# An early x1 buffer for the last block of the finished batch, one gap more per block, and another bank for the first feed-forward product

## The chip, the cores and the metric

The kernel runs on one core of a Trainium2 chip. The metric is the device time of one execution in microseconds. Before the change three runs took 2745.36, 2745.53 and 2747.55 us; the median is 2745.53 us. One further execution, of 2746.23 us, was recorded by the profiler, and everything that is read from a profile below is read from that one.

## The reference

Two batches of 512 channels by 2048 tokens (64 x 32 positions), all in fp32, go through two layers.

```python
x = conv_attention(x)                      # layer 0: softmax attention, 8 heads of 64, + residual
t = tokens(x)
t = t + attn(norm(t))                      # layer 1: Nystrom attention, 256 landmarks
t = t + ffn(norm(t))                       # two linear maps 512 -> 512, no nonlinearity between

# attn, per head: qL, kL are means of 8 tokens each of q and k
attn1 = softmax(q @ kL.T); attn2 = softmax(qL @ kL.T); attn3 = softmax(qL @ k.T)
z = pinv(attn2, 6 iterations)              # xz = a @ z; z = z/4 @ (13 I - xz (15 I - xz (7 I - xz)))
out = attn1 @ (z @ (attn3 @ v)) + conv33(v)
out = out @ Wout + bout
```

The kernel works with channels on the partitions and tokens along the free axis. The two maps of the feed-forward are multiplied into one matrix `mT` beforehand.

## The kernel before

**Stages.** The first half (to about 1500 us) is layer 0; then come the projections of layer 1. From 1733 us a loop goes over eight pairs of heads, `todo`: the four pairs of batch 1 (n = 0 to 3) and then the four of batch 0 (n = 4 to 7). For each pair it runs six iterations of the pseudo-inverse, `Pair.pinv`. This chain is narrow and every step waits for the one before: a transpose of one block on TensorE (line 1528), a copy of it by ScalarE (L1529), eight matmul passes (L1538), two VectorE steps (L1551) that make the next operand. Two heads alternate, so that one head's matmuls run under the other's VectorE steps.

**Turns.** Between the iterations, `pinv` calls `chunk(0)` to `chunk(4)` (called c0 to c4 here), and in the last iteration `last(0)` to `last(5)` (l0 to l5). These calls put other work in: attn1 of the pair before, attn3 and values of the pair after, and the work that ends batch 1. This last work is one generator, `finish1_units`, and each `advance(finish)` moves it by one unit; below, one such call is a *turn*. The generator goes over four blocks of 512 tokens. For each block it emits, turn by turn:

- the load of x1 (the residual) for the block, issued on GpSimd's queue (L1644) into the only buffer of tag `xr`, and two turns that do nothing (`gap(2)`; the load takes the first);
- out.0 to out.3: 8 matmul passes each of the output projection (L968) and one VectorE addition into x1 (L975);
- s0, two VectorE additions (L986, L987), a gap; s1, the mean on TensorE (L990) and its subtraction on VectorE (L991); s2, three squares on ScalarE (L994, L997); s3, three VectorE additions (L1002, L1003), a gap; s4, the variance on TensorE (L1006), its root on ScalarE and the reciprocal on VectorE (L1660);
- map.0 to map.3: 8 matmul passes each of the feed-forward (L1694); the VectorE steps and the store of the result (L1683 to L1685, called rest) come a turn later than their product, and rest.3 runs at the head of the next block's load.

**Order.** TensorE, VectorE, ScalarE and GpSimd each execute in the order in which the Python code emits. Only the order of SyncE's queue, which issues most DMAs, is chosen by the scheduler. An instruction that waits holds up all that follows on its engine.

**The last stage.** After the loop a string gives the order by hand: `1` is a unit of attn1 of the last pair (`last_attn1`), `f` a turn of `finish`, `n` makes the four blocks of batch 0 and issues the loads of their x1 on SyncE, `a`/`b` are their output projections, `s`/`t` the steps of their norms. `n` takes the buffers of batch 1's outputs, and so comes after out.3 of batch 1's last block. Then the blocks of batch 0 go through the feed-forward, their products in banks chosen by `wide_banks`: products 0 and 2 in the two banks of their own, `side_bank(1)` and `side_bank(3)`, products 1 and 3 in the two of `product_bank`. `side_bank(1)` is also the bank of attn1's values (L1611), which L1631 reads.

**Buffers.** PSUM has four banks for general use (`bank`), two `product_bank`, and `side_bank` 1 and 3. In SBUF the tag `v` of `kvpool` has two buffers, used in turn for the keys and the values of the pairs. The values of pair 7, the last, are read for the last time by its convolution, in c4 of pair 6.

Of the kernel before, what the change touches and what calls it, by code (L numbers as in the profile page):

```python
# [10 lines left out]
F32 = mybir.dt.float32  # L11
# [5 lines left out]
P = 128  # L17
# [4 lines left out]
NPAIR = HEADS // 2  # L22
TB = 512
NTB = S // TB
NST = S // P
# [638 lines left out]
def fast_path(  # L664
# [43 lines left out]
    lpool = ctx.enter_context(tc.tile_pool(name="l1", bufs=1))  # L708
    both = ExitStack()
    xpool = both.enter_context(tc.tile_pool(name="x1", bufs=NTB))  # L710
    kvpool = both.enter_context(tc.tile_pool(name="kv1", bufs=2))
# [19 lines left out]
    def bank(name):  # L731
        return ps.tile([P, 512], F32, tag="pp", name=name)
# [11 lines left out]
    def side_bank(i, name):  # L744
        return ps.tile([P, 512], F32, tag=f"av{i}", name=name, bufs=1)

    def product_bank(name):
        return ps.tile([P, 512], F32, tag="pr", name=name, bufs=2)
# [5 lines left out]
    def block_of(pool, tag, name):  # L754
        return pool.tile([P, KC, TB], F32, tag=tag, name=name)
# [37 lines left out]
    def advance(gens, n=1):  # L793


        made, i = 0, 0
        while made < n and i < len(gens):
            got = next(gens[i], gens)
            if got is gens:
                gens.pop(i)  # L800
            elif got is GAP:
                i += 1
            else:
                made += 1
        return made

    def drain(gen):
        for _ in gen:
            pass

    def gap(n=1):
        for _ in range(n):
            yield GAP
# [45 lines left out]
    class Heads0:  # L859
# [61 lines left out]
        def values(self):  # L921
            for t in range(NTB):
                values_of_tokens(self.v, t, self.xbs[t], lambda k: wv_sb[:, k, self.cols], self.name)
                yield
# [107 lines left out]
    def finish0_units(b, oTs, outs_done):  # L1032
        last = None
        for t in range(NTB):
            xb = block_of(lpool, "xr", f"xr_f0_{b}_{t}")
            nc.sync.dma_start(xb, chunked(x[b])[:, :, t * TB : (t + 1) * TB])
            yield from gap()

            for m, _ in enumerate(out0_units(b, t, xb, oTs)):
                if last and m == 0:  # L1040
                    next(last)
                yield
            if t == NTB - 1:
                outs_done.append(True)
            if last:
                yield from gap()
            xn = block_of(lpool, "xn", f"xn_f0_{b}_{t}")
            last = norm0_steps(b, t, xb, xn, xn[:, :2, :])
            next(last)
            yield from gap(2)  # L1050
            next(last)
            yield
            yield from gap(2)
            next(last)
            yield from gap(2)
            next(last)
            yield
        next(last)
# [155 lines left out]
    class Pair:  # L1214
# [310 lines left out]
        def flip(self, X, name):  # L1525
# [3 lines left out]
            nc.scalar.copy(X[:, 1, :P], tp[:, :P])  # L1529

        def pinv(self, chunk, last):


# [167 lines left out]
                yield  # L1701
            rest(*last)

    def finish1_units(b, os):
        for t in range(NTB):
            xb = block_of(lpool, "xr", f"xb_g_{b}_{t}")
            f = Finish1(b, t, os, xb, lambda: block_of(lpool, "xn", f"xn_g_{b}_{t}"), True)
            yield from gap(2)
            yield from f.out_units()
            yield from f.norm_units()  # L1710
            yield from f.map_units(lambda m, name: bank(name))


    todo = [(b, hp) for b in range(B) for hp in range(NPAIR)]
# [3 lines left out]
    oTs, finish, work = [], None, []  # L1718
    for n, (b, hp) in enumerate(todo[:-1]):
# [14 lines left out]
        finish = None  # L1734
# [6 lines left out]
        if hp == NPAIR - 1:  # L1741
            outs_done = []
            finish = finish0_units(b, oTs, outs_done)
# [47 lines left out]
    b = B - 1  # L1791

    def as_block(tile):
        return tile.rearrange("p a b -> p (a b)").rearrange("p (k n) -> p k n", k=KC)
# [60 lines left out]
    todo = pairs[1] + pairs[0]  # L1855
# [28 lines left out]
    def late_buffer(name):  # L1884

        return block_of(xpool, "xb", name).rearrange("p k n -> p (k n)")
# [33 lines left out]

    finish = []
    for n, pair in enumerate(todo):
        before = todo[n - 1] if n else None
        after = todo[n + 1] if n + 1 < len(todo) else None
        if n + 2 < len(todo):
            todo[n + 2].prefetch_w()
        if n == NPAIR + 2:
            before.load_o(kvpool.tile([P, S], F32, tag="k", name=f"o2_{n - 1}"))  # L1930
        if n == NPAIR + 3:
            before.load_o(late_buffer(f"o2_{n - 1}"))
        pair.iteration_start()
        while vals:
            advance(vals)
        if after:
            after.prefetch()
            after.attn3_begin()
        if n + 2 < len(todo):
            vals = [values(n + 2)]  # L1940
        if n:
            q = late_buffer if n > NPAIR + 1 else lambda name: kvpool.tile([P, S], F32, tag="k", name=name)
            pair.prefetch1(q(f"q2_{pair.name}"))

        def chunk(c):
            nonlocal landmarks
            if before and 0 < c <= n_ones:
                before.attn1_end(c - 1)
            if n == NPAIR and c == 1:

                finish.append(finish1_units(1, [p.o for p in todo[:NPAIR]]))
            advance(finish)
            if c == NTB:
                if after:
                    landmarks = after.landmarks_values()
                    next(landmarks)
                    drain(convolution(n + 1))
                else:
                    advance(finish, 2)
                return  # L1960
            ones_before = before if c < n_ones else None
            if ones_before:
                if c:
                    before.attn1_scores(c, 0)
                    before.attn1_scores(c, 1)
                before.attn1_add(c)
            if after:
                for s, bank_of in ((2 * c, product_bank), (2 * c + 1, bank)):
                    after.attn3_scores(s, bank_of)
                    after.attn3_add(s)  # L1970
            else:
                advance(finish)
            if ones_before:
                before.attn1_values(c)
            if after:
                after.attn3_values(2 * c)
            else:
                advance(finish)
            if ones_before:
                before.attn1_sums(c)  # L1980
            if after:
                after.attn3_values(2 * c + 1)
            if ones_before:
                before.attn1_inverse(c)
            if n == NPAIR + 2 and c % 2:
                advance(finish)

        def last(i):
            nonlocal start
            if i == 1 and after:  # L1990
                next(landmarks)
                drain(landmarks)
                start = after.start_values()
            if i == 2 and after:
                next(start)
            else:
                advance(vals)
            if i == 3 and after:
                next(start)
            if n_ones < NTB:  # L2000

                if i == 0:
                    before.attn1_scores(n_ones, 0)
                    before.attn1_scores(n_ones, 1)
                    before.attn1_add(n_ones)
                if i == 1:
                    before.attn1_values(n_ones)
                if i == 2:
                    before.attn1_sums(n_ones)
                if i == 3:  # L2010
                    before.attn1_inverse(n_ones)
                if i == 5:
                    before.attn1_end(n_ones)
            if i == 5:
                pair.attn1_scores(0, 0)
                pair.attn1_scores(0, 1)
            advance(finish)

        landmarks = start = None
        n_ones = NTB if n + 2 < len(todo) else NTB - 1  # L2020
        pair.pinv(chunk, last)

    def last_attn1():
# [15 lines left out]
            yield  # L2039

    def wide_banks(m, name):
        return product_bank(name) if m % 2 else side_bank(1 + m, name)

    def last_block(t):
        xb = as_block(qopool.tile([P, NST, P], F32, tag="qo", name=f"xb_g_0_{t}"))
# [16 lines left out]


    ones_last = last_attn1()
    for c in "11ffnf11f1ff1afafff1f1f1f1faas11bs1bs1bbt":
        if c == "f":
            advance(finish)
        elif c == "n":

            fs = [last_block(t) for t in range(NTB)]  # L2070
            outs = [f.out_units() for f in fs]

            st = [f.steps(deviation_of(t)) for t, f in enumerate(fs)]
        else:
            next(ones_last if c == "1" else {"a": outs[0], "b": outs[1], "s": st[0], "t": st[1]}[c])
# [104 lines left out]
```

## Time and profile before

| | us |
|---|---|
| median of three runs | 2745.53 |
| profiled execution, whole | 2746.23 |
| its span from first to last instruction | 2744.4 |
| TensorE busy | 2698.0 (98%) |
| VectorE busy | 1631.3 (59%) |
| ScalarE busy | 905.5 (33%) |
| GpSimd busy | 161.1 (6%) |

TensorE is busy nearly all the time, so what can be lost or won lies in its short idle stretches, and in the stretches in which its clock is halved. Times in the text are us from the start of the span. Pair 6 starts at 2351 and pair 7 at 2458; the string of the last stage starts at 2574.

### The profile page before, as it was taken

The numbers are of one execution on the slowest core, as the hardware profiler recorded it, in microseconds if no ns is written. First come the engines' busy times: TensorE is split into PE (matmuls) and PEld (weight loads), VectorE is DVE, ScalarE is ACT, GpSimd is POOL, SyncE is SP. The second block draws the span as 40 slices with busy tenths as digits, with TensorE's granted clock in tenths as the row PEclk, the third lists the DMA queues.
The fourth block names the chain that finished last, engine by engine and source line by source line (L and its number), as shares of the span: only waits on it lengthen the run. The fifth ranks groups of instructions, "written<-read, shape, count | busy, mean of one in ns | idle before, by whom it ended". The sixth has DMA issues, their size and how long they took to land.

```text
span 2744.4 us, 41181 instructions
## 1 busy us (share of the span) xinstructions
PE 2698.0 (98%) x16994; PEld 1361.6 (50%) x16994; DVE 1631.3 (59%) x2087; ACT 905.5 (33%) x1352; POOL 161.1 (6%) x109
## 2 busy tenths in 40 slices
PE   9999999999999999999999999999999999998899
PEld 5343443434443334343344455777677666655334
DVE  3768777665558755657667544544644645465455
ACT  1434343433335334445422223233333222221210
POOL 0101101000011100000002000000000000000000
PEclk9999999999999999999999999999999999999999
DMA  4100000212111200012024632213111213020311
GB/s 146 43 9 24 28 20 24 85 36 70 32 66 54 96 24 21 24 41 74 24 88 172 208 122 90 96 34 114 57 36 59 63 41 105 24 70 27 104 39 47
DMA packets 111476, 173.99 MB, mean 63 GB/s; under 512 B 16176, under 2 KB 67888, under 8 KB 106672
## 3 DMA queue, kind: packets, MB, share of 16 engines
q1 hardware_dynamic: 105136, 150.00, 16.8%
q0 software_dynamic: 5440, 20.97, 2.1%
q8 instruction: 135, 2.21, 0.3%
q14 instruction: 61, 0.50, 0.1%
q10 hardware_dynamic: 704, 0.31, 0.0%
HBM read 90.87 MB, written 63.57 MB: 56 GB/s over the span
## 4 chain that ended last, share of the span: by engine, by line
PE 90%; DVE 5%; DMA 2%; SPq 1%; ACT 1%; issue 1%; POOL 0%; DVEq 0%; POOLq 0%; ACTq 0%
PE sc_f L1072 15%; PE av_f L1102 15%; PE pp L1245 8%; PE pb L1538 5%; PE pa L1538 5%; PE vp_f L953 4%; PE vp L953 4%; PE fp_g L1694 4%; PE pp_k_f L905 4%; PE yp_f L968 4%; PE pp_q_f L905 3%; PE yp_g L968 3%; PE sc L1367 2%; PE av L1388 2%; PE sc L1595 2%; DVE acc_f L1090 2%
## 5 line engine op out<-in xcount | busy, mean ns | idle before, releaser
L1090 DVE TENSOR_TENSOR acc_f<-acc_f,p_f 128x1024 f32<-128x1024 f32 x448 | 582.3, 1300 | 209.0 <-ACT p_f L1080 180.4
L1080 ACT ACTIVATE p_f<-sc_f 128x1024 f32<-128x1024 f32 x512 | 496.4, 1021 | 564.2 <-PE sc_f L1072 561.5
L1072 PE MATMUL sc_f<-q_f,k_f 64*64 64x512 f32 x4096 | 491.1, 595 | 2.7 <-ACT p_f L1080 2.7
L1102 PE MATMUL av_f<-p_f,v_f 64*64 64x512 f32 x4096 | 484.3, 589 | 0.0
L1102 PEld LDWEIGHTS av_f<-p_f,v_f 64*64 64x64 f32 x4096 | 156.5, 133 | 283.1 <-issue 283.1
L1072 PEld LDWEIGHTS sc_f<-q_f,k_f 64*64 64x64 f32 x4096 | 145.8, 133 | 285.6 <-issue 262.0
L1245 PE MATMUL pp<-xh,w 128*128 128x512 f32 x512 | 229.1, 600 | 0.7 <-ACT q L1248 0.7
L1245 PEld LDWEIGHTS pp<-xh,w 128*128 128x128 f32 x512 | 95.3, 191 | 121.0 <-issue 113.8
L1538 PE MATMUL pb<-R 128*128 128x192 f32 (+1 forms) x640 | 151.9, 384 | 2.1 <-DVE M L1551 2.1
L1538 PE MATMUL pa<-M 128*128 128x192 f32 (+1 forms) x640 | 150.7, 380 | 1.4 <-ACT M L1529 1.4
L953 PEld LDWEIGHTS vp_f<-wv_f,x 128*128 128x128 f32 x1024 | 115.7, 192 | 13.5 <-issue 11.8
L1538 PEld LDWEIGHTS pb<-R 128*128 128x128 f32 x640 | 108.2, 193 | 25.9 <-DVE M L1551 3.1
L953 PE MATMUL vp<-w,xh 128*128 128x128 f32 x1024 | 120.9, 276 | 0.0
L953 PEld LDWEIGHTS vp<-w,xh 128*128 128x128 f32 x1024 | 117.0, 192 | 7.2 <-issue 4.6
L1538 PEld LDWEIGHTS pa<-M 128*128 128x128 f32 x640 | 108.1, 193 | 21.6 <-ACT M L1529 4.2
L953 PE MATMUL vp_f<-wv_f,x 128*128 128x128 f32 x1024 | 118.8, 277 | 0.0
L968 PE MATMUL yp_g<-o,wo_f 128*128 128x512 f32 x256 | 116.4, 604 | 2.3 <-DVE xb_g L975 2.3
L1694 PE MATMUL fp_g<-xn_g,mT 128*128 128x512 f32 (+1 forms) x264 | 114.4, 583 | 3.2 <-DVE rinv L1631 3.2
L905 PE MATMUL pp_k_f<-x,wk_f 128*128 128x512 f32 x256 | 114.3, 599 | 1.4 <-DVE k_f L908 1.0
L905 PE MATMUL pp_q_f<-x,wq_f 128*128 128x512 f32 x256 | 114.2, 598 | 1.3 <-DVE q_f L908 1.3
L968 PE MATMUL yp_f<-q_f,wo_f 128*128 128x512 f32 x256 | 113.6, 598 | 0.8 <-DVE xr_f L975 0.8
L1120 POOL TENSOR_TENSOR q_f<-q_f,rinv_f 128x512 f32<-128x512 f32 x32 | 46.3, 1445 | 1041.8 <-DMA rinv_f<-acc_f 829.6
(198 smaller groups left out, 2710.4 us busy)
## 6 DMA issues: line engine op xcount, KB each, us to landing
xh<-xh_fd SPq DMA_DIRECT2D x12, 1024.0 KB, 5.4
rinv_f<-acc_f SPq DMA_DIRECT2D x256, 32.0 KB, 1.9
xr_f<-in_x_dram SPq DMA_DIRECT2D x8, 1024.0 KB, 5.4
x_fd<-xr_f POOLq DMA_DIRECT2D x8, 1024.0 KB, 4.9
xh_fd<-xn_f POOLq DMA_DIRECT2D x8, 1024.0 KB, 4.7
k_fd<-k SPq DMA_DIRECT2D x32, 256.0 KB, 2.9
q_fd<-q SPq DMA_DIRECT2D x32, 256.0 KB, 2.8
k<-k_fd SPq DMA_DIRECT2D x8, 1024.0 KB, 6.2
```

The source lines that it names most:

```text
L905: nc.tensor.matmul(pp, lhsT=w_sb[kind][:, k, cols], rhs=xbs[t][:, k, :], start=k == 0, stop=k == KC - 1)
L953: nc.tensor.matmul(vp[:, j * P : (j + 1) * P], lhsT=xb[:, k, j * P : (j + 1) * P], rhs=w_of(k), start=k == 0, stop=k == KC - 1,)
L968: nc.tensor.matmul(yp, lhsT=wo_sb[:, k, m * P : (m + 1) * P], rhs=oTs[k][:, toks], start=k == 0, stop=k == NPAIR - 1,)
L1072: nc.tensor.matmul(sc[r * D : (r + 1) * D, h, :], lhsT=hd.k[rows, lo : lo + D], rhs=hd.q[rows, t * TB : (t + 1) * TB], start=True, stop=True,)
L1080: nc.scalar.activation(p, sc, AF.Exp, scale=D**-0.5)
L1090: nc.vector.tensor_tensor(acc, first if c == 1 else acc, p, ALU.add)
L1102: nc.tensor.matmul(av[r][half, :], lhsT=hd.v[keys, c, half], rhs=pp[keys, h, :], start=c == 0, stop=c == NST - 1,)
L1245: nc.tensor.matmul(pp, lhsT=self.w[j][:, c, :], rhs=xhs[t][:, c, :], start=c == 0, stop=c == KC - 1)
L1367: nc.tensor.matmul(scs[h][:, j * LM : (j + 1) * LM], lhsT=self.k[rows, c * P : (c + 1) * P], rhs=self.L[0][rows, :], start=True, stop=True,)
L1388: nc.tensor.matmul(self.av3[half, :LM], lhsT=self.v[:, c, half], rhs=self.p3[s][:, h, j * LM : (j + 1) * LM], start=c == 0, stop=c == NST - 1,
L1538: nc.tensor.matmul(dst, lhsT=lhsT[:, k, t * P : (t + 1) * P], rhs=rhs[:, k, :], start=k == 0, stop=k == 1)
L1694: nc.tensor.matmul(fp[:, cols], lhsT=mT[:, k, m * P : (m + 1) * P], rhs=self.xn[:, k, cols], start=k == 0, stop=k == KC - 1,)
```

## The change

It has four parts.

1. At the start of pair 7 a buffer of the tag `v` is taken and the x1 of batch 1's last block (block 3) is loaded into it, on GpSimd's queue. When `finish1_units` comes to block 3, it uses this buffer, and neither loads nor waits.
2. Blocks 1 and 2 have `gap(3)` instead of `gap(2)` after their load. The four gaps and loads of all blocks together take as many turns as before (block 3 has two fewer).
3. The string of the last stage has one `f` more, at its second place.
4. `wide_banks` gives products 0 and 2 to `product_bank`, 1 and 3 to `side_bank(1)` and `side_bank(3)`.

```diff
-    def finish1_units(b, os):
+    def finish1_units(b, os, early):
         for t in range(NTB):
+            if t == NTB - 1 and early:
+                f = early.pop()
+                yield from f.out_units()
+                yield from f.norm_units()
+                yield from f.map_units(lambda m, name: bank(name))
+                return
             xb = block_of(lpool, "xr", f"xb_g_{b}_{t}")
             f = Finish1(b, t, os, xb, lambda: block_of(lpool, "xn", f"xn_g_{b}_{t}"), True)
-            yield from gap(2)
+            yield from gap(3 if t else 2)
...
         if n == NPAIR + 3:
+
+            xb = as_block(kvpool.tile([P, NST, P], F32, tag="v", name="xb_g_early"))
+            xn = lambda: block_of(lpool, "xn", "xn_g_early")
+            early.append(Finish1(1, NTB - 1, [p.o for p in todo[:NPAIR]], xb, xn, True))
             before.load_o(late_buffer(f"o2_{n - 1}"))
...
-                finish.append(finish1_units(1, [p.o for p in todo[:NPAIR]]))
+                finish.append(finish1_units(1, [p.o for p in todo[:NPAIR]], early))
...
     def wide_banks(m, name):
-        return product_bank(name) if m % 2 else side_bank(1 + m, name)
+        return side_bank(m, name) if m % 2 else product_bank(name)
...
-    for c in "11ffnf11f1ff1afafff1f1f1f1faas11bs1bs1bbt":
+    for c in "1f1ffnf11f1ff1afafff1f1f1f1faas11bs1bs1bbt":
```

Because the generator is one sequence, a gap that is put in moves all that follows by a turn. This is where the units fall, from the first turn that differs (1.out.0 is the first output projection of block 1; `-` is a turn without work; the turns of one call are parted by bars):

| turn | before | after |
|---|---|---|
| pair 5, l4, l5 | 1.out.0, 1.out.1 | -, 1.out.0 |
| pair 6, c0 | 1.out.2 | 1.out.1 |
| c1 | 1.out.3 \| 1.s0 | 1.out.2 \| 1.out.3 |
| c2 | - | 1.s0 |
| c3 | 1.s1 \| 1.s2 | - \| 1.s1 |
| c4 | 1.s3 | 1.s2 |
| l0, l1, l2 | -, 1.s4, 1.map.0 | 1.s3, -, 1.s4 |
| l3, l4, l5 | 1.map.1, 1.map.2, 1.map.3 | 1.map.0, 1.map.1, 1.map.2 |
| pair 7, c0 | load of block 2 \| - \| 2.out.0 | 1.map.3 \| load of block 2 \| - |
| c1 | 2.out.1 \| 2.out.2 \| 2.out.3 | - \| 2.out.0 \| 2.out.1 |
| c2 | 2.s0 \| - \| 2.s1 | 2.out.2 \| 2.out.3 \| 2.s0 |
| c3 | 2.s2 \| 2.s3 \| - | - \| 2.s1 \| 2.s2 |
| c4 | 2.s4 \| 2.map.0, 2.map.1 | 2.s3 \| - |
| l0, l1, l2 | 2.map.2, 2.map.3, load of block 3 | 2.s4, 2.map.0, 2.map.1 |
| l3, l4, l5 | -, 3.out.0, 3.out.1 | 2.map.2, 2.map.3, 3.out.0 |
| string, to `n` | 1 1 3.out.2 3.out.3 | 1 3.out.1 1 3.out.2 3.out.3 |

From `n` on every unit stands where it stood. In c3 of pair 7 attn1 and attn3 have nothing to do, so the turns stand there alone.

More of the change, by code (lines that the diff above doesn't have):

```diff
@@ L1919, in fast_path @@
     todo[0].prefetch1(kvpool.tile([P, S], F32, tag="k", name="q2_first"))
-    finish = []
+    finish, early = [], []
     for n, pair in enumerate(todo):
```

## The prediction

> **What bounds the kernel now.** TensorE is busy for 98% of the span, so I look for its idle stretches. First, who it waited for between 2450 and 2660 us (us in total, times, longest):
>
> ```profile
> PE p_pb L1528 <- DVE R L1551: 5.4, 2, 3.7
> PE fp_g L1694 <- DVE rinv L1631: 3.2, 1, 3.2
> PE yp_g L968 <- DVE xb_g L975: 2.3, 1, 2.3
> ```
>
> Then the timeline around the longest and the third, which are the loads of blocks 2 and 3 of batch 1:
>
> ```profile
> 2470.74 0.77 POOL L1644 DMA_DIRECT2D xb_g<-x_fd  x1 [16.58 <-DMA out_dram<-xb_g]
> ...
> 2476.39 0.75 DVE L975 SCALAR_TENSOR_TENSOR xb_g<-yp_g,b_f,xb_g 128x512 f32<-128x512 f32 x1 [7.56 <-DMA xb_g<-x_fd]
> ...
> 2478.72 0.69 DVE L1551 SCALAR_TENSOR_TENSOR R<-M,pa 128x320 f32<-128x320 f32 x2
> ...
> 2560.59 0.77 POOL L1644 DMA_DIRECT2D xb_g<-x_fd  x1 [33.24 <-DMA out_dram<-xb_g]
> ...
> 2568.11 0.75 DVE L975 SCALAR_TENSOR_TENSOR xb_g<-yp_g,b_f,xb_g 128x512 f32<-128x512 f32 x1 [8.21 <-DMA rinv<-acc]
> 2568.91 5.40 PE L968 MATMUL yp_g<-o,wo_f 128*128 128x512 f32 x8 [2.35 <-DVE xb_g L975]
> ```
>
> x1 lands late, VectorE stands in L975, and the pseudo-inverse's L1551 (block 2) or the next projection's bank (block 3) stands behind it. The second wait names another DMA, but 7.5 us after the load's issue, against 5.65 for block 2, I read it as x1. Last, four stretches: length, TensorE busy, ..., granted clock, DMA:
>
> ```profile
> 2475.47:2486.06 10.59, 6.42 (x20) 4.92 (x19) 5.75 (x12) 0.53 (x2) 0.00 (x0) 0.68 0.12 28
> 2515.15:2533.67 18.52, 15.65 (x77) 11.83 (x73) 14.55 (x28) 5.58 (x13) 1.64 (x1) 1.00 0.06 15
> 2566.56:2574.24 7.68, 5.33 (x9) 2.03 (x9) 1.74 (x4) 0.64 (x2) 1.25 (x1) 0.78 0.02 5
> 2646.11:2653.80 7.69, 4.53 (x11) 1.82 (x10) 6.62 (x5) 0.69 (x1) 1.26 (x1) 1.00 0.10 25
> ```
>
> A clock of 0.68 over 10.59 us is half speed for 6.8 us, 0.78 over 7.68 for 3.4: each long wait is paid twice.
>
> [...] 2.35 us of idleness was enough, while 3.16 (at 2647) was not[...]. [...]
>
> **The change part by part.**
>
> *Gains.* (a) Block 2's load. After the last store of block 1 is issued (2467.72) x1 is usable at 2476.39, 8.7 us later. In the new order that store comes 1.65 us after 1.map.3's product (0.05 + y 0.68 + addition 0.69 + 0.2), so x1 is there at +10.3; 2.out.0's L975 comes after attn1's values 1.9, its sums 0.6, an iteration 7.45, scores 2.0 and the product 3.6, at +15.7. The wait goes, with 5.4 us to spare. The stretch 2475.47 to 2486.06 needs 2 x 1.84 = 3.7 us: gain 6.9.
> (b) Block 3's load. The early buffer's last reader ended at about 2429, and GpSimd is free at 2454.2, after its addition at 2452.90 (1.26): one issue of 0.77 us, and 5.65 us later, near 2460, x1 is there, 100 us before use. GpSimd's next work, block 2's load, comes 10 us later. SyncE loses nothing and gains nothing by it; its stores of results move with their rest units, a turn or two later. 2566.56 to 2574.24 held one product of 3.6: gain 4.05.
> (c) Iterations 3 and 4 of pair 7. 2515.15 to 2533.67 is 18.5 us for two iterations of 7.45: 3.6 lost because L991, then L1002 and L1003, stood ahead of L1551; with 0.34 ahead of the mean (2513.11), 3.9. These units leave that place: gain 3.9, and what takes their place is charged below.
> (d) The bank. Product 0 of the last stage waits for L1631 to read `side_bank(1)`:
>
> ```profile
> 2649.45 0.69 DVE L1631 TENSOR_TENSOR rinv<-av,rinv 128x512 f32<-128x512 f32 x1 [0.40 <-DMA rinv<-acc]
> ...
> 2650.29 3.67 PE L1694 MATMUL fp_g<-xn_g,mT 128*128 128x512 f32 x8 [3.16 <-DVE rinv L1631]
> ```
>
> `product_bank` has been free since the pseudo-inverse; product 1, now in `side_bank(1)`, comes 4.6 us after product 0 starts, later than L1631's end at 2650.1. TensorE runs without a hole from there to the end, and VectorE's chain keeps up (L991 would start at 2653.4, the additions for the variance end near 2659.5, wanted at 2661.8): gain 3.16.
> (e) Small holes of 0.46 (2391.38), 0.46 (2544.80) and 0.38 (2557.71) lose their cause: 1.2, of which I count 0.8.
> Sum 18.8.
>
> *Losses.* (f) Pair 6, l0. Before:
>
> ```profile
> 2434.49 1.23 DVE L1604 TENSOR_TENSOR acc<-p,p 128x1024 f32<-128x1024 f32 x1 [5.79 <-ACT p L1600]
> 2435.63 0.48 DVE L1551 SCALAR_TENSOR_TENSOR R<-M,tp 128x128 f32<-128x128 f32 x2
> 2435.76 1.13 PE L1006 MATMUL var_g<-sq_g,mean_w 128*128 128x512 f32 x2
> 2436.82 1.08 PE L1513 MATMUL wp<-M,R 128*64 128x256 f32 x8
> ```
>
> Now 1.s3's additions (1.29 + 0.69, about 2.0) are emitted between L1604 and L1551. R is ready at 2438.1 instead of 2436.1, and the variance that filled TensorE is gone: it stands from 2435.76 to 2438.2, 2.45. [...] I take 0.8.
> (g) Pair 6, l2 to l3. 1.s4 in l2: variance ends 3.3 us after wp starts, ScalarE's table 1.28 and root 0.69 end at 4.95, L1660 takes 3.35 and L1551 0.48 behind it, R at 8.8. TensorE has the transposes and one product, to 7.5: 1.4.
> (h) Pair 7, c3, the largest. 2.s1 and 2.s2 follow each other with no other work. With TensorE's end of iteration 3 at 0: mean to 1.0; VectorE does L1631 first (it waits for the spread of the sums, 6.35 us after its reciprocal as in before, to about 1.9), then L991's 2.29, to 4.2. ScalarE's squares wait for that and take 2.15, to 6.4; the copy of iteration 4's first block stands behind them, to 6.75. TensorE is through the half that needs no copy at 2.0: 4.75 us idle. Before shows the mechanism, smaller, at pair 5's start:
>
> ```profile
> 2228.22 1.06 ACT L994 ACTIVATE sq_g<-xn_g 128x1024 f32<-128x1024 f32 x1
> 2229.16 1.15 ACT L997 ACTIVATE sq_g<-xn_g 128x512 f32<-128x512 f32 x2
> 2230.20 0.26 ACT L1529 COPY M<-p_pa 128x128 f32<-128x128 f32 x1
> 2230.52 0.81 PE L1538 MATMUL pa<-M 128*128 128x320 f32 x2 [1.43 <-ACT M L1529]
> ```
>
> [...] Loss 6.45, bounds 4.75 and 8.1.
> (i) Pair 7, c4 has no TensorE work now; the last transpose waits for L1551 of the last product (0.1 + 0.75): 0.75; and 2.s4 in l0 puts L1660 ahead of L1551, covered by 2.map.0 but for 0.4. Loss 1.15.
> Sum 3.25 + 1.4 + 6.45 + 1.15 = 12.25. The moved products themselves cost what they cost before; 1.map.3 and 3.out.1 only change pair or stage. From `n` on SyncE's 16 loads and all else keep their places.
>
> Net 18.8 - 12.25 = 6.6 us, 0.24%: the profiled 2746.23 becomes 2739.7, the median 2745.53 becomes **2738.9**.
>
> **Rivals.** *The new waits stay hidden*: if c3's squares do not hold up the copy, (h) is gone: 2738.9 - 6.45 = 2732.4; with none of (f) to (i), 2726.7. For it: loads are the longest waits in the trace. Against: 2230.20 above. *The stalls only move*: (f) and (h) throttle two windows each and SyncE's chosen order, which I cannot see, delays a spread by one DMA group (4.94 us for 8 issues, of which 1 to 2 reach TensorE): 3 to 5 us more, 2742 to 2744, no measurable change. For it: c3's wait is longer than the one it replaces. *Slower*: the clock does not come back. [...] Without throttle charges the net gain is 9.1; each halved 3.4 us costs 1.7; slower by 5.5 us takes 9 windows, 30 us of half clock: 2751. Against: both halvings of before ended after one or two windows.
>
> **How the numbers follow.** 0.2% is 5.5 us, about what a measurement of this kernel can tell from no change: under 2740.0 is faster. Main case 2736 to 2741.5: 0.53, of which 0.4 below 2740. New waits hidden, 2726 to 2736: 0.20. Stalls only move, to 2745: 0.20. Slower: 0.07. Faster 0.60, same 0.33, slower 0.07. Leaving out the slow tail and the lower half of the hidden case gives 2731 to 2744.
>
> **What would show it.** Right: no VectorE wait for x1 near 2475 or 2565; no wait of L1694 for L1631; a TensorE wait of 4 to 5 us at L1538 for ScalarE's copy in pair 7, then clock 0.5; one of 2.4 us at L1513 near 2436. Wrong: squares off ScalarE's path, L975 still waiting, or the product waiting for another bank.

## The result and the profile after

The changed kernel takes 2738.94 us (median of 9 runs, 2737.89 to 2741.36), the kernel before 2746.61 us beside it (9 runs, 2743.16 to 2749.18). The ratio is 0.9975 with a 95% interval of 0.9967 to 0.9983: faster by 0.25%, and 2738.9 was predicted. The profiled execution took 2739.02 us with a span of 2737.2 us, against 2746.23 and 2744.4 before. It was 2.4 us behind that of before when it came to the changed part (the same hole of 1.44 us begins at 2231.50 instead of 2229.08), with 3.4 us of half clock at 33.3 us (behind a hole of 2.40 us) that before does not have. So of the 7.2 us between the spans the changed part gained 9.6.

Who TensorE waited for between 2450 and 2660 us in the kernel after (us in total, times, longest):

```profile
PE pa L1538 <- ACT M L1529: 4.6, 1, 4.6
...
PE p_pa L1528 <- DVE M L1502: 1.0, 1, 1.0
PE tp_M L1528 <- DVE M L1551: 0.5, 1, 0.5
```

The three lines shown of before (L1528 for R, L1694 for `rinv`, L968 for `xb_g`) are gone. In their place one wait stands at the head: a matmul pass of the pseudo-inverse waits for ScalarE's copy.

The loads of x1, in the timeline of the kernel after (start, duration, engine, operation, idle time before it and what ended that):

```profile
2460.52 0.77 POOL L1644 DMA_DIRECT2D xb_g_early<-x_fd  x1
...
2477.31 0.75 POOL L1644 DMA_DIRECT2D xb_g<-x_fd  x1 [16.03 <-DMA out_dram<-xb_g]
...
2488.30 0.75 DVE L975 SCALAR_TENSOR_TENSOR xb_g<-yp_g,b_f,xb_g 128x512 f32<-128x512 f32 x1 [1.07 <-PE yp_g L968]
```

Block 2's first L975 comes 11.0 us after its load was issued and now waits for its own product only. The trace shows its landing 6.3 us after the issue, near 2483.6, 4.7 us ahead of that use. The early load of block 3 is issued in the same stretch, more than 100 us before it is used (its L975 runs at 2567.2).

The longest wait of the kernel after, in pair 7, c3, where 2.s1 and 2.s2 follow each other:

```profile
2522.34 0.69 DVE L1631 TENSOR_TENSOR rinv<-av,rinv 128x512 f32<-128x512 f32 x1 [0.75 <-DMA rinv<-acc]
2522.95 2.28 DVE L991 TENSOR_TENSOR xn_g<-xb_g,mean_g 128x2048 f32<-128x2048 f32 x1
...
2525.26 1.06 ACT L994 ACTIVATE sq_g<-xn_g 128x1024 f32<-128x1024 f32 x1 [5.83 <-DVE xn_g L991]
2526.23 1.13 ACT L997 ACTIVATE sq_g<-xn_g 128x512 f32<-128x512 f32 x2
2527.26 0.24 ACT L1529 COPY M<-p_pa 128x128 f32<-128x128 f32 x1
...
2527.56 1.44 PE L1538 MATMUL pa<-M 128*128 128x320 f32 x2 [4.59 <-ACT M L1529]
```

The transpose that the copy reads was done at 2521.77. ScalarE was idle for 5.83 us, the last 3.5 of them with this transpose done, yet it did not copy: the squares stood ahead in its queue and waited for L991. The stretch around it (length, busy time of TensorE, its weight loads, VectorE, ScalarE and GpSimd, granted clock, DMA) shows that the wait is paid twice here too, 0.69 over 10.88 us being half speed for 6.8 us (2.6 of them fell into the wait itself):

```profile
2521.25:2532.13 10.88, 6.29 (x20) 4.33 (x19) 4.64 (x8) 2.51 (x5) 1.27 (x1) 0.69 0.01 3
```

The other new waits, in pair 6's last iteration:

```profile
2437.93 1.29 DVE L1002 TENSOR_TENSOR sq_g<-sq_g,sq_g 128x512 f32<-128x512 f32 x2
2439.25 0.69 DVE L1003 TENSOR_TENSOR sq_g<-sq_g 128x512 f32<-128x512 f32 x1
...
2440.20 1.28 PE L1513 MATMUL wp<-M,R 128*64 128x256 f32 x8 [2.06 <-DVE R L1551]
...
2445.38 3.35 DVE L1660 RECIPROCAL rstd_g<-rstd_g 128x512 f32<-128x512 f32 x1 [5.04 <-ACT rstd_g L1008]
...
2449.02 1.18 PE L1513 MATMUL wp<-M,R 128*64 128x256 f32 x8 [1.19 <-DVE R L1551]
```

And at the start of pair 7, one that the prediction did not charge:

```profile
2448.98 1.75 DVE L1624 RECIPROCAL acc<-acc 128x256 f32<-128x256 f32 x1
...
2450.79 4.95 SPq L790 DMA_DIRECT2D rinv<-acc  x8
...
2458.54 0.69 DVE L1631 TENSOR_TENSOR rinv<-av,rinv 128x512 f32<-128x512 f32 x1 [3.97 <-DMA rinv<-acc]
2459.15 0.68 DVE L1683 TENSOR_TENSOR y_g<-fp_g,rstd_g 128x512 f32<-128x512 f32 x1
...
2459.86 1.26 DVE L1684 TENSOR_TENSOR xb_g<-y_g,xb_g 128x512 f32<-128x512 f32 x1
...
2461.53 0.30 PE L1528 MATMUL p_pa<-ident,M 128*128 128x128 f32 x1 [1.00 <-DVE M L1502]
```

VectorE waited 3.97 us for the spread of the sums (the DMA `rinv<-acc`), the result of 1.map.1 (L1683, L1684) stood behind it, and the first step of pair 7's pseudo-inverse (L1502) behind that. The same order, a result between L1631 and L1502, stands there before the change, without a wait. What is new is that the reciprocal of the sums (L1624) comes late: it stands behind L1660 and L1551, and ends 1.7 us after TensorE began the pair's last product of L1513 (2449.02), where before it ended 1.4 us ahead of that product (2445.36 against 2446.77). The eight spreads were issued right behind it.

### The profile page after: what moved, and what is told of

It reads as the page before. It is cut to its first block, busy times and chain, and to the rows that moved or that the text cites. A ratio compares the mean times of both kernels' runs of the same rounds, so it can differ in the third digit from the quotient of the medians.

```text
span 2737.2 us, 41174 instructions
## 1 busy us (share of the span) xinstructions
PE 2695.4 (98%) x16994; PEld 1361.0 (50%) x16994; DVE 1631.7 (60%) x2087; ACT 906.3 (33%) x1352; POOL 162.0 (6%) x109
## 4 chain that ended last, share of the span: by engine, by line
PE 91%; DVE 5%; DMA 1%; ACT 1%; SPq 1%; issue 1%; POOL 0%; DVEq 0%; ACTq 0%; POOLq 0%
PE sc_f L1072 15%; PE av_f L1102 15%; PE pp L1245 8%; PE pa L1538 5%; PE pb L1538 5%; PE vp_f L953 4%; PE vp L953 4%; PE pp_k_f L905 4%; PE yp_g L968 4%; PE yp_f L968 4%; PE fp_g L1694 4%; PE pp_q_f L905 3%; PE av L1388 2%; PE sc L1367 2%; PE sc L1595 2%; PE av L1611 2%
## 5 line engine op out<-in xcount | busy, mean ns | idle before, releaser
L968 PE MATMUL yp_g<-o,wo_f 128*128 128x512 f32 x256 | 114.8, 597 | 0.0
L968 PE MATMUL yp_f<-q_f,wo_f 128*128 128x512 f32 x256 | 113.5, 598 | 0.8 <-DVE xr_f L975 0.8
L1551 DVE SCALAR_TENSOR_TENSOR R<-M,pa 128x320 f32<-128x320 f32 (+1 forms) x160 | 59.9, 416 | 67.8 <-PE pa L1538 67.8
```

The source lines that it names most:

```text
L968: nc.tensor.matmul(yp, lhsT=wo_sb[:, k, m * P : (m + 1) * P], rhs=oTs[k][:, toks], start=k == 0, stop=k == NPAIR - 1,)
L1551: nc.vector.scalar_tensor_tensor(out, m, scale, pr, ALU.mult, ALU.subtract)
```

## The experiments

The theory under test: the loads of x1 out of the way, the undisturbed iterations and the bank give what the prediction says in (a) to (d), and the moved turns take two thirds of it back, most of it in (h). The rivals: the new waits cost nothing or other amounts, and the gains are smaller. Each ratio is against the kernel before, run beside it (median 2745.43 us of 33 runs beside the bank alone, block 3's load alone and the two variants of the changed kernel's gaps; 2744.1 us of 13 runs beside the other four). Medians that were measured beside different runs of before can differ by a microsecond or two for that reason alone: before took 2746.61 us beside the changed kernel, and 2745.43 and 2744.1 us here. All kernels compute the whole reference.

### The bank alone

The kernel before with this edit only:

```diff
-        return product_bank(name) if m % 2 else side_bank(1 + m, name)
+        return side_bank(m, name) if m % 2 else product_bank(name)
```

> The kernel before with the banks of the last stage alone exchanged. The theory of the prediction (term d): TensorE no longer waits 3.16 us for L1631 ahead of the first product of the last stage, nothing else takes its place, and the time falls by 3.2 us to about 2743.4 (ratio 0.9988). The rival: VectorE's chain (L1660, L991) sets this stage, the wait comes back a few us later ahead of a mean or a variance, and the time stays within 1 us.

Measured: 2740.91 us (21 runs), ratio 0.9983 (0.9977 to 0.9990). The wait of L1694 is gone from its profile. That is 4.5 us by the medians; the interval, 2.7 to 6.3 us, holds the predicted 3.16. More of it is the halved clock, which can follow this hole, as the next kernel shows: the record has the mean granted clock of every run, and over the runs it was 0.9969 for before and 0.9973 here, which is 1.2 us less lost to half speed (0.001 of the clock over the span is 2.7 us).

### The early load of block 3 alone

The kernel before with part 1 of the change, but with `gap(2)` kept ahead of block 3, so that every turn stays in its place:

```diff
+            if t == NTB - 1 and early:
+                f = early.pop()
+                yield from gap(2)
+                yield from f.out_units()
...
         if n == NPAIR + 3:
+            xb = as_block(kvpool.tile([P, NST, P], F32, tag="v", name="xb_g_early"))
+            xn = lambda: block_of(lpool, "xn", "xn_g_early")
+            early.append(Finish1(1, NTB - 1, [p.o for p in todo[:NPAIR]], xb, xn, True))
```

> The kernel before with the early load of block 3 alone: its two gaps are kept, so every unit stays in its turn. The theory (term b): L975's wait of 8.2 us near 2568 was for x1; it goes, with TensorE's 2.35 us and the halved clock behind it, and the time falls by 4.05 us to about 2742.6 (ratio 0.9985). The rival: the trace named another DMA, the spread of the sums; if that one was waited for, the wait stays and the time does not change.

Measured: 2746.53 us (13 runs), ratio 0.9998 (0.9989 to 1.0006). The expected gain did not come, though the wait did go. From the timeline of this kernel:

```profile
2565.98 0.75 DVE L975 SCALAR_TENSOR_TENSOR xb_g_early<-yp_g,b_f,xb_g_early 128x512 f32<-128x512 f32 x1 [3.14 <-PE yp_g L968]
...
2569.38 0.69 DVE L1631 TENSOR_TENSOR rinv<-av,rinv 128x512 f32<-128x512 f32 x1 [2.26 <-DMA rinv<-acc]
```

L975 no longer waits for a DMA, and the spread that the profile of before names as its releaser is waited for by L1631, three microseconds later. So the wait of 8.21 us in the profile of before was one for x1, as the prediction read it; that trace also has the landing of x1, 7.3 us after its issue at 2560.59, which is 0.2 us ahead of L975. The time went elsewhere. The stretch around the untouched hole of the bank, in the same execution:

```profile
2644.80:2655.00 10.20, 7.04 (x11) 3.02 (x11) 5.85 (x4) 0.69 (x1) 1.26 (x1) 0.67 0.05 13
```

The hole is the same 3.16 us, but here the clock is halved for 6.8 us after it; in the profile of before it stayed at 1.00. A further 3.4 us of half clock follow the hole at 2528.9. The two executions together: holes of 2.35 and 0.68 us (3.0) less, and 17.1 instead of 10.2 us of half clock, which is about 3.4 us more. The runs lie apart in the same way, six from 2740.6 to 2744.5 and seven from 2746.5 to 2749.1, and the granted clocks on record say that the halved clock does it: the seven have 0.995 or 0.996, the six 0.996 (two of them) to 0.998. The mean of the 13 is 0.9960 against 0.9969 for before, 2.5 us more lost to half speed; the mean time is still 0.8 us under before's. Together that is 3.3 us, near the 3.0 of the holes that went. So the load's waits were worth their holes, and the half clock took most of that back. Why more runs of this kernel had it is not shown.

### The early load of block 3 and the bank

To see the load without that hole, both edits above together:

> The kernel before with the early load of block 3 and the exchanged banks, every unit in its turn of before. The early load alone brought 0.02% where 0.15% was expected, although its waits are gone from the trace; there the hole of 3.16 us at the last stage's first product was followed by 6.8 us of halved clock, which the kernel before did not have in its profile. If the early load is worth its removed holes (2.35 and 0.68 us) and the halving is chance, then without that hole it shows: 3 to 4 us under the banks alone, about 2737.5 against 2740.9. The rival: the early load costs something elsewhere, and the time stays at the banks' 2740.9.

Measured: 2738.74 us (9 runs), ratio 0.9975 (0.9965 to 0.9984). That is 2.2 us under the bank alone by the medians and by the ratios, and the intervals overlap. The mean clocks of the two are alike (0.9974 and 0.9973), so this is the price of the holes alone: 2.7 us less idle time between the two profiles. So (b) is worth 2 to 3 us and not 4.05. The ratio is also that of the whole change, 0.9975. This kernel has parts 1 and 4 of the change and none of its moved turns, so the moved turns, with the wait for block 2's load that they take away, gave back what they gained, to within the 2 or 3 us of the intervals. In the profile of the bank alone the hole that it removes is smaller than in that of before (2.35):

```profile
2569.00 2.41 PE L968 MATMUL yp_g<-o,wo_f 128*128 128x512 f32 x5 [1.47 <-DVE xb_g L975]
```

x1 was used there 6.5 us after GpSimd took up the load, instead of 7.5, and no clock was halved. These are two executions; which of them is the usual one in this place is not known.

### Two, two and four gaps

The changed kernel with the extra gap of block 1 moved to block 2. Pair 6 then runs as before, and from block 2's first product on all stands as in the changed kernel. This tests (f) and (g):

```diff
-            yield from gap(3 if t else 2)
+            yield from gap(4 if t == 2 else 2)
```

> The changed kernel with gaps of 2, 2, 4 turns in place of 2, 3, 3: block 1 is back in the turns of before, block 2 stays where the change put it. The theory (terms f and g): the waits of 2.06 and 1.19 us at L1513 in pair 6 and of 1.00 us at pair 7's start go, a hole of 0.46 us comes back, and the time is 3.5 to 4 us under the changed kernel's, about 2735.2. The rival: these waits come from something else than block 1's turns, and the time stays at 2738.9.

Measured: 2734.61 us (5 runs), ratio 0.9962 (0.9948 to 0.9975), 4.3 us under the changed kernel. The holes of 2.06, 1.19 and 1.00 us are gone. One of 0.46 comes back and one is new, where c0 of pair 7 no longer has a product:

```profile
2469.11 0.64 PE L779 MATMUL rs<-acc,ones 128*32 128x256 f32 x8 [1.44 <-DVE acc L1604]
```

The wait of (h) is 4.86 us here. The holes sum to -4.25 + 0.46 + 1.44 + 0.26 = -2.1 us; the half clock, which began in this execution only as the wait ended, cost TensorE 3.4 us of work at half speed instead of 4.3, another -0.4. From the hole near 2230 to the end the two profiles lie 3.0 us apart, so that these 2.5 us are most of it. Of the 4.3 us between the medians, 1.2 lie between the kernels before that ran beside the two. So the waits of (f), (g) and the start of pair 7 are caused by the extra gap of block 1, but the time settles their price only to 2 us or so.

### One gap between the mean and the squares

The changed kernel with one gap between s1 and s2 of block 2, and one `f` more in the string so that what follows `n` keeps its place. This tests (h):

```diff
+            if (self.b, self.t) == (1, 2):
+                yield GAP
...
-    for c in "1f1ffnf11f1ff1afafff1f1f1f1faas11bs1bs1bbt":
+    for c in "1ff1ffnf11f1ff1afafff1f1f1f1faas11bs1bs1bbt":
```

> The changed kernel with one empty turn between the mean and the squares of block 2, so that the squares stand in c4 of pair 7 and not ahead of the copies of its last iteration; one more turn in the string makes up for it. The theory (term h): the wait of 4.6 us of L1538 for ScalarE's copy goes, with the halved clock (6.8 us) behind it, and the time is 6.3 us under the changed kernel's, about 2732.6. The rival: the squares then hold up the copies of the last transposes in c4, and half or more of it, 3 us, comes back at L1513: 2735.5 to 2736.

Measured: 2732.72 us (5 runs), ratio 0.9951 (0.9937 to 0.9965), 6.2 us under the changed kernel. The wait for the copy is gone. L991 still stands ahead of L1551, and this costs holes of 1.10 and 0.60 us; a third, of 0.79, is new at 2553.65:

```profile
2521.53 2.28 DVE L991 TENSOR_TENSOR xn_g<-xb_g,mean_g 128x2048 f32<-128x2048 f32 x1
...
2524.26 0.33 PE L1528 MATMUL p_pb<-ident,R 128*128 128x128 f32 x1 [1.10 <-DVE R L1551]
```

So the squares right behind L991 are the cause of (h): with L991 alone TensorE stands 1.7 us in this place, with the squares behind it 4.6. The holes of the two profiles differ by only -4.60 + 1.10 + 0.60 + 0.79 = -2.1 us, with 3.4 us of half clock in place of the 4.3, -0.4; from the hole near 2230 to the end they lie 2.7 us apart, which this explains. The profiled execution, of 2734.33 us, was the slowest of the five, 1.6 us over their median, and 1.2 of the 6.2 us lie between the kernels before that ran beside the two. That 2732.72 came so near the expected 2732.6 is therefore luck in part: the expectation left out that L991 alone still costs 1.7 us here. The time alone gives (h) no closer than to 2 or 3 us.

### Both loads early, the turns of before

If the loads and not the turns bring the gain, the loads can be made early and the turns left alone. Block 2's x1 goes early into the freed `v` buffer, and block 3's into the `xr` buffer as soon as block 1 has left it. The gaps and the string are those of before, the bank is the new one:

```diff
+            if t < 2 or not early:
                 xb = block_of(lpool, "xr", f"xb_g_{b}_{t}")
                 f = Finish1(...)
+            else:
+                f = early.pop(0)
+                if t == 2:
+                    xb3 = block_of(lpool, "xr", f"xb_g_{b}_3")
+                    early.append(Finish1(b, 3, os, xb3, ...))
             yield from gap(2)
```

> Every unit in its turn of before, banks exchanged, and both loads early: block 2's into the buffer of tag v at pair 7's start, block 3's into xr as soon as block 1 has left it. The theory: what the change gains (terms a, b, d: 6.9, 3 to 4, 3.2 to 4.6) comes from the loads and the bank and needs no moved turn, so the terms f, g and h are not paid and c is not gained: about 2745.4 - 14 = 2731.5. The rival: block 2's projection in its old turn meets another wait behind x1, and the time is not under 2736.

Measured: 2731.49 us (5 runs), ratio 0.9948 (0.9934 to 0.9963). It differs from the kernel with block 3's load early and the new bank (2738.74) by block 2's load in the main: 7.25 us for (a), where 6.9 was predicted. The two profiles have 4.1 us less idle time and 2.9 us less lost to half speed between them, 6.9 in all. Its timeline has the load 17 us ahead of its use:

```profile
2454.72 0.77 POOL L1644 DMA_DIRECT2D xb_g_early<-x_fd  x1
...
2471.73 0.75 DVE L975 SCALAR_TENSOR_TENSOR xb_g_early<-yp_g,b_f,xb_g_early 128x512 f32<-128x512 f32 x1 [2.29 <-PE yp_g L968]
```

With the turns of before it is already 7.4 us faster than the changed kernel by the medians.

### Both loads early, the additions of the squares moved

What was left of (c), holes of 1.66 and 0.60 us behind L1002 and L1003 and 3.4 us of half clock, is taken out by two more gaps behind s2 of block 2. Block 3 then needs no gap ahead of it, since it waits for no load:

```diff
-            yield GAP
+            yield from gap(3 if (self.b, self.t) == (1, 2) else 1)
...
-            yield from gap(2)
+            yield from gap(0 if t == 3 else 2)
...
-    for c in "11ffnf11f1ff1afafff1f1f1f1faas11bs1bs1bbt":
+    for c in "1f1ffnf11f1ff1afafff1f1f1f1faas11bs1bs1bbt":
```

> As the run with both loads early, and block 2's three additions (L1002, L1003) moved out of c3 into c4 of pair 7 by two empty turns more after its squares, with block 3's two gaps left out for them. The theory: the waits of 1.69 and 0.60 us of iteration 4 (term c) go, those of 0.34 and 0.59 stay, and the last turns have a product each: 2.5 to 3.5 us under that run, about 2728.5. The rival: the reciprocal of the deviation (L1660), now in l0, holds up L1551 and gives it back: no difference.

Measured: **2727.24 us** (5 runs), ratio 0.9937 (0.9922 to 0.9952): 0.63% faster than before, and 0.4% under the changed kernel by the medians and by the ratios. In its profile the clock is not halved once between 1498 and 2723 us. Who TensorE still waited for between 2200 and 2720 us, longest first:

```profile
PE av L1611 <- DVE rinv L1631: 1.6, 1, 1.6
PE var_g L1006 <- DVE sq_g L1003: 1.5, 1, 1.5
```

### The same with another string

The last stage's order again, to take out these two holes:

```diff
-    for c in "1f1ffnf11f1ff1afafff1f1f1f1faas11bs1bs1bbt":
+    for c in "1f1ffn1f1f1ff1afaafff1f1f1f1fas11bs1bs1bbt":
```

> As the last, with two units moved in the string of the last stage: attn1's next scores ahead of block 3's first additions (so that L1631 comes before L986 and L987), and one output projection of batch 0 ahead of block 3's variance. The theory: the wait of 1.56 us of L1611 for L1631 shrinks to about 0.3 and the one of 1.50 us of L1006 for L1003 goes: 2 to 2.8 us less, about 2726. The rival: the moved projection is missed where it stood, and a hole opens there: no difference.

Measured: 2727.16 us (4 runs), ratio 0.9933 (0.9916 to 0.9951). It can't be told from the kernel above. The hole of 1.56 us became 0.61 and that of 1.50 went, but one of 0.78 appeared, where the mean waits for the additions of s0: 1.67 us less idle time in all, inside the scatter of the runs.

## Why the prediction was right

The net was right (6.6 us predicted; 0.25% of 2745.5 us is 6.9), and so was the mechanism: every wait named as going went, and the largest new one appeared in its place at its size. That the net came out so close is luck in part, since errors of terms cancel. The sizes of the terms, from the holes of the profiles and the differences of medians:

| step | predicted, us | shown, us | by |
|---|---|---|---|
| (a) block 2's load | 6.9 | 7.25 | both loads early against block 3's, with the bank in both |
| (b) block 3's load | 4.05 | 2 to 3, less where the half clock followed another hole | that load with the bank, against the bank |
| (c) iterations 3 and 4 | 3.9 | 3.2 of idle time gone | profiles before and after (0.34 + 0.59 + 1.69 + 0.60) |
| part of (c) and (e) | | 4.25: 2.6 idle, 1.7 of clock | additions moved, against not |
| (d) the bank | 3.16 | 4.5 | the bank alone |
| (f) 1.s3 ahead of L1551 | 2.45 | 2.06, the added 0.8 of clock not | profile after |
| (g) L1660 ahead of L1551 | 1.4 | 1.19 | profile after |
| start of pair 7 | none | 1.00 | profile after |
| (h) squares ahead of the copy | 6.45 | 6.7: 4.60 idle, 2.1 of clock | profile after (half clock from 2527.56, the end of the wait, to 2531.82: 4.3 / 2) |
| (i) c4 and l0 | 1.15 | 0.47 | profile after |

As steps between medians, from before over the bank, block 3's load and block 2's to the last kernel but one, the gains are 4.5, 2.2, 7.25 and 4.25 and sum to 18.2 us (17.3 by that kernel's ratio to before). The prediction had 18.8, 0.8 of it for the small holes of (e), of which 0.46 and 0.38 went in the last step; its three holes sum to 1.3 and not 1.2. What (f) and (h) have on top of their holes, 0.8 and 1.7 us, was the author's estimate from before, where 3.4 us of half clock, 1.7 us of lost work, followed the hole of 2.35 us; 0.8 is half of that. The last step comes near (c) by chance: its 1.7 us of clock was not charged in (c), and the holes of 0.34 and 0.59 stay in it. The losses, holes and in (h) the clock, sum to 2.06 + 1.19 + 1.00 + 6.7 + 0.47 = 11.4 us (12.25 predicted). The changed kernel and the last but one differ in little but these (the 0.47 is in both), and lie 2738.94 - 2727.24 = 11.7 us apart by the medians, 10.4 by the ratios. Between 2200 and 2720 us the two profiles differ by 7.8 us of idle time and 2.1 of clock, 9.9 in all.

**Where sizes were off.** (b) and (d) were each read from one hole of one execution. The hole of (b) was a long one with a halved clock, that of (d) one without, and the errors of -1.9 and +1.3 us cancel in part.

An estimate takes the clock out: from each run's time, the part of the span that its mean granted clock lacks is subtracted, and the mean taken. Before then comes to 2737.4 us, the bank alone to 2733.9, block 3's load alone to 2734.1, both to 2731.3 and both loads early to 2727.6. That is 3.5 us for (d), 3.3 for (b) alone and 2.6 beside the bank, 3.7 for (a), near their holes of 3.16, 3.0 and 3.7. So the holes were read well, and what comes on top for the clock is what one profile can't tell.

The start of pair 7 is a step left out in (f) and (g): these follow L1551 behind L1660, but not the reciprocal of the sums behind both, whose spread L1631 and then L1502 wait for. The prediction priced a late spread only as a rival ("one DMA group", from SyncE's order); here the spread began late because its reciprocal did, and it cost 1.0 us. (i) was too high by 0.7 and (f) by 1.2, so that with the missed 1.0 the losses came out only 0.8 too high.

**The working of (a)** held by its steps. 1.map.3's product ended at about 2472.8, the load was issued 4.5 us and L975 ran 15.5 us after it, where 15.7 was predicted for L975. x1 landed at 10.8, where 10.3 was predicted.

**The working of (h)** held by its steps: mean 1.02, L1631 to 1.4 us after the mean's end (0.9 predicted), L991 2.28, squares 1.06 and 1.13, the copy behind them. This was to be had from two lines of the profile of before, L1529 behind L997 at 2230, and the order of the turns. That an instruction which waits holds up what follows on its engine is seen most plainly here: ScalarE stood idle for 5.83 us, for 3.5 of them ahead of a copy whose input was ready.

**The rivals.** *New waits hidden* (2726.7 to 2732.4): they were not hidden; the time it gives is that of the kernels in which the turns stay (2731.49) or are moved without (f) to (h) (2727.24). *The stalls only move*: partly so, 11.4 of 18.2 us. *Slower*: the clock came back after 6.8 us, two of what the prediction calls windows, at 2531.8, and behind the holes of (f), (g), (i) and the start of pair 7 (2.06, 1.19, 0.47 and 1.00 us) it stayed at 1.00.

## What to carry to other kernels

A late load is cured by loading early into a free buffer; moving the turns of work to give the load time costs what the moved work holds up: here the moved turns won (a) and (c), some 11 us, and lost as much, and the kernel without them is as fast (2738.74 us). With both loads early and the turns left alone it is 2731.49. In a chain that crosses in-order engines, look for each moved operation which step of the chain is emitted behind it on the same engine, and what the moved operation itself waits for: three squares that waited for VectorE held up a copy of 0.24 us by 5.5. A gain read from one hole of one profile is uncertain by the halving of the clock that may or may not follow (none or 6.8 us of it behind the same hole of 3.16 us here); where it decides, look at several executions and at the granted clock of each.

## What was not expected of the hardware

Whether the clock is halved behind a hole of 2 to 3.5 us differs from one execution to the next. Behind the 3.16 us at the bank it stayed at 1.00 before (2646.11 to 2653.80) and was halved for 6.8 us in the kernel with block 3's load early alone (0.67 over 2644.80 to 2655.00). Behind 2.35 us it was halved for 3.4 us before, behind 2.06 us it stayed at 1.00 after. So the length of the hole alone does not decide it.

The profiles of before and after show where the clock was at 0.50:

| profile | half clock, us from the start of the span | length, us |
|---|---|---|
| before | 1494.9 to 1498.3 | 3.41 |
| | 2477.9 to 2484.8 | 6.83 |
| | 2570.1 to 2573.5 | 3.41 |
| | 2740.8 to the end | 3.6 |
| after | 33.3 to 36.7 | 3.41 |
| | 1497.6 to 1501.0 | 3.41 |
| | 2525.0 to 2531.8 | 6.83 |
| | 2733.2 to the end | 4.0 |

The starts lie 983.04, 92.16 and 170.67 us apart before, which is 288, 27 and 50 times 3.4133 us, and 1464.32, 1027.41 and 208.21 us after, 429, 301 and 61 times. Counted in such steps of 3.413 us, the first of them begins 3.27 us after the start of the span before and 2.54 after. Ahead of the last step, six steps at full clock in these two profiles held 2.03 to 3.07 us of TensorE's idle time, and half clock followed each; those with 1.69 us or less were followed by full clock. Of the eight steps at half clock, two held idle time (1.71 and 2.56 us) and were followed by another, and six held none and were followed by full clock. By this count the hole of 3.16 us at the bank was cut before into 1.47 and 1.69 us, and no half clock followed. That the same steps decide it in the other kernels is not shown.

In the runs of before too the granted clock and the time go together. Of the 33, the nine at 0.998 took 2742.3 to 2744.8 us, the 13 at 0.997 took 2744.3 to 2747.7, the ten at 0.996 took 2746.1 to 2749.9, and the one at 0.995 took 2751.6. So most of the spread of a few microseconds between runs goes with the halved clock. What halved the clock in the runs without a profile is not shown.
